# A GpSimd drain inside the routed loop of a long-convolution and mixture-of-experts kernel

## The chip, the core and the metric

The kernel runs on one core of a Trainium2 chip. A core has TensorE (PE in the profile; its weight loads are PEld), VectorE (DVE), ScalarE (ACT), GpSimd (POOL) and SyncE (SP), each with its own queue of instructions, and 16 DMA engines that all queues share. The metric is the time of the whole program on the device in microseconds (us), the median of several runs.

## What is computed

The input `x` holds 128 sequences of 32 heads, each 512 long. Each head is convolved with its own kernel, made from a state-space model, and masked to the length of its sequence. The 4096 rows that result go through a gated feed-forward layer with 16 experts of which each row uses 4, plus a shared expert that all rows use. The sum is added to `x`.

```python
y = irfft(rfft(u, n=2 * L) * rfft(K, n=2 * L)[None])[..., :L] + u * D[:, None]
y = y * mask                                    # rows of 512, 128 x 32 of them
scores = sigmoid(y @ gate_w.T) + bias
topk_w, topk_idx = top_k(scores, 4)             # normalised to a sum of one
out = sum over experts e of  cw[e] * (silu(y @ Wg[e].T) * (y @ Wu[e].T)) @ Wd[e].T
out = out + (silu(y @ Sg.T) * (y @ Su.T)) @ Sd.T
result = x + out
```

## The kernel before

The work has three stages. In the first, the convolution runs head by head on TensorE; its rows go to a table `y_rows` in HBM, and GpSimd copies `x` into `out` with 8 large transfers (line 865). In the second, the shared expert runs over 8 units of 512 rows; GpSimd adds the results into `out` with 32 indirect transfers (line 953), while VectorE works out which row goes to which expert.

The third stage is the routed loop, in which the change lies. The rows chosen for each expert are packed into tiles of 128. There are at least `NT_MIN` = 128 tiles and at most `NT` = 143; the number depends on the data, and steps from 130 on stand inside nested branches (`rest`) that are left when no tile is left. With the data of these runs, 134 tiles are computed. `turn_of(step)` writes the order of one step by hand:

- GpSimd issues the gather of the rows of tile `step + 4` from `y_rows` into one of 6 buffers `yg` (`gather`, line 894).
- TensorE transposes the rows of tile `step` (`tokens`, line 1022); ScalarE copies them out of PSUM into `yt`.
- SyncE reads whether tile `step - 2` is the first of an expert. If it is, SyncE waits until all adds issued so far have landed (line 1107), because two experts can add to the same row; then it sets a mark (`order`, line 1110).
- TensorE multiplies tile `step - 1` with the expert's gate and up weights (`inner`, line 1054) and tile `step - 2` with its down weights (`outer`, line 1080); ScalarE and VectorE do the gate in between.
- VectorE copies the result into one of 5 buffers `ob` (line 1089), and GpSimd issues an indirect transfer that adds its rows into `out` (line 1090), once the mark of the tile is set.
- SyncE issues a conditional load of an expert's weights into a ring of 8 places (line 880), for a tile six steps on.

So GpSimd's queue in this loop is an add, a gather, an add, a gather, and so on, in the order written, with nothing else between. All of its transfers are described by software on GpSimd; each one has a semaphore that tells of its landing, and the instructions that read or overwrite the data wait for that semaphore. The build closes every program with drains on all engines and a barrier between them (line 1212 in the profile), and opens it in the same way (line 1201).

The order around the change is this:

```python
turn_of(0)
unit_step(NU)
for step in range(1, NT_MIN + 2):
    turn_of(step)
```

Of the kernel before, what the change touches and what calls it, by code (L numbers as in the profile page):

```python
# [55 lines left out]
AHEAD = 4  # L56
NT = (B * H * TOPK - E) // P + E
NT_MIN = B * H * TOPK // P
QC = P // KT
WSZ = 2 * KT * I + IT * L  # L60

# [14 lines left out]
def ssm_moe_kernel(  # L76
# [15 lines left out]
    nc = tc.nc  # L92
# [39 lines left out]

    gw = const.tile([P, KT, QC], F32, tag="gw", name="gw")
    nc.gpsimd.memset(gw, 0.0)
# [24 lines left out]
    gather_q = const.tile([P, E], F32, tag="gather_q", name="gather_q")  # L159
    nc.gpsimd.tensor_add(gather_q, ident[:, :E], ident[:, QC : QC + E])  # L160
    for kt in range(2, KT):
        nc.gpsimd.tensor_add(gather_q, gather_q, ident[:, kt * QC : kt * QC + E])

# [378 lines left out]
    def gates(tb):  # L542
# [7 lines left out]
        for kt in range(KT):  # L550
            mm = nc.tensor.matmul(
                parts[kt * QC : (kt + 1) * QC],
                lhsT=gw[:, kt, :],
# [287 lines left out]
    def dep(of, on, why):  # L841
        tc.add_manual_dep(of.ins, on.ins.name, SYNC, reason=why)
# [36 lines left out]
    def load_expert(e, dst, cond=None):  # L879
        return nc.sync.dma_start(  # L880
            out=dst, in_=w_all[bass.ds(e, 1)].rearrange("o p w -> p (o w)"), cond=cond
        )
# [10 lines left out]
    def gather(t):  # L893
        nc.gpsimd.indirect_dma_start(  # L894
            out=at(yg, t),
            out_offset=None,
            in_=y_rows[:, :],
            in_offset=bass.IndirectOffsetOnAxis(ap=made["get"][:, t : t + 1], axis=0),
        )
# [71 lines left out]
    def unit_step(u):  # L971


        nonlocal gathered
        if u < NU:
            k_us[u] = nc.tensor.value_load(k_u[0:1, u : u + 1], min_val=1, max_val=KT)
            for it in range(IT):
                up(u, it, p_g, 0)
                if u == 0 and it == 0:
                    sums(NB - 1)  # L980
                    route(NB // RB - 1)
                nc.scalar.activation(sgu[it], p_g[it], AF.Silu)
                up(u, it, p_u, I)
                nc.vector.tensor_mul(at(zu, u)[:, it, :], sgu[it], p_u[it])
                if u > 0 or it > 0:
                    next(making, None)
        if u == 0:
            weights_out(NB // RB - 1)
        for q in range(TU // P):
            if u > 0:  # L990
                down(u - 1, q)
                if q % 2 == 1:
                    next(making, None)
        while "get" in made and gathered < AHEAD:
            gather(gathered)
            gathered += 1
        while "lexp0" in made and len(loads) < R - 1 and free_after(len(loads)) <= u:
            j = len(loads)
            e = nc.sync.value_load(made["lexp0"][0:1, j : j + 1], min_val=0, max_val=E - 1)
            loads.append(load_expert(e, ring_flat[:, j * WSZ : (j + 1) * WSZ]))  # L1000
# [15 lines left out]
    def tokens(t):  # L1016

        pt = at(p_t, t)

        def transposes(n):  # L1020
            for q in range(KT - n, KT):
                nc.tensor.transpose(pt[:, q, :], at(yg, t)[:, q * P : (q + 1) * P], ident)  # L1022

        if t < len(p_t):
            transposes(KT)
        else:
            by_tiles(k_ts[t], transposes)
        nc.scalar.copy(at(yt, t), pt)  # L1028
        nc.vector.scalar_tensor_tensor(  # L1029
            at(junks, t),  # L1030
            epos,
            made["texp"][:, t : t + 1],
            at(yg, t)[:, L:],
            ALU.is_equal,
            ALU.mult,
            accum_out=at(wts, t),
        )
# [6 lines left out]
    def registers(t):  # L1044
        w0s[t] = nc.tensor.value_load(
            made["woff"][0:1, t : t + 1], min_val=0, max_val=(R - 1) * WSZ
        )
        k_ts[t] = nc.tensor.value_load(made["ntk"][0:1, t : t + 1], min_val=1, max_val=KT)

    def inner(t):  # L1050
        pgu = at(p_gu, t)
        def products(n):
            for q in range(KT - n, KT):
                mm = nc.tensor.matmul(  # L1054
                    pgu,
                    lhsT=at(yt, t)[:, q, :],
                    rhs=ring_flat[:, bass.ds(w0s[t] + q * 2 * I, 2 * I)],
                    start=(q == KT - n),
                    stop=(q == KT - 1),
                )  # L1060
                in_ring(t, mm)

        by_tiles(k_ts[t], products)
        sg = at(sgs, t)
        nc.scalar.activation(sg, pgu[:, :I], AF.Silu)  # L1065
        nc.vector.scalar_tensor_tensor(  # L1066
            at(zs, t), pgu[:, I:], at(wts, t), sg, ALU.mult, ALU.mult
        )

    def turn(t):  # L1070
        for it in range(IT):
            nc.tensor.transpose(  # L1072
                at(p_z, t)[:, it, :], at(zs, t)[:, it * P : (it + 1) * P], ident
            )
        nc.vector.tensor_copy(at(zts, t), at(p_z, t))  # L1075

    def outer(t):
        po = at(p_o, t)
        for it in range(IT):
            mm = nc.tensor.matmul(  # L1080
                po,
                lhsT=at(zts, t)[:, it, :],
                rhs=ring_flat[:, bass.ds(w0s[t] + WD + it * L, L)],
                start=(it == 0),
                stop=(it == IT - 1),
            )
            in_ring(t, mm)
        ob = at(obs, t)
        nc.vector.tensor_copy(ob, po)  # L1089
        add = nc.gpsimd.indirect_dma_start(  # L1090
            out=out,
            out_offset=bass.IndirectOffsetOnAxis(ap=made["put"][:, t : t + 1], axis=0),
            in_=ob,
            in_offset=None,
            compute_op=ALU.add,
        )
        dep(add, marks[t], "the rows it adds to")
        for other in adds:
            tc.declare_no_dep(add.ins, other.ins, reason="other rows, or behind the mark")
        adds.append(add)  # L1100

    def order(t):


        new = nc.sync.value_load(made["fresh"][0:1, t : t + 1], min_val=0, max_val=1)  # L1105
        with tc.If(new > 0):
            wait = nc.sync.nop()
            for other in adds:
                dep(wait, other, "the rows they add to")
        marks[t] = nc.sync.nop()  # L1110

    with tc.manual_schedule(engines=None):

        dep(nc.tensor.nop(), parts_last[0], "in TensorE's order")
        for u in range(NU):
            unit_step(u)
        for _ in making:
            pass
        registers(0)

        def turn_of(step):
            if step + AHEAD < NT:
                gather(step + AHEAD)
            else:
                nc.gpsimd.nop()
            if step < NT:
                tokens(step)
            if step >= 2:
                order(step - 2)
                turn(step - 2)  # L1130
            if 1 <= step <= NT:
                inner(step - 1)
            if step >= 2:
                outer(step - 2)
            if step + 1 < NT:
                registers(step + 1)
            if 1 <= step < NT:

                t = step - 1
                e = nc.sync.value_load(made["lexp"][0:1, t : t + 1], min_val=0, max_val=E - 1)  # L1140
                to = nc.sync.value_load(made["loff"][0:1, t : t + 1], min_val=0, max_val=(R - 1) * WSZ)  # L1141
                go = nc.sync.value_load(made["load"][0:1, t : t + 1], min_val=0, max_val=1)  # L1142
                ld = load_expert(e, ring_flat[:, bass.ds(to, WSZ)], go)
                for other in loads:
                    tc.declare_no_dep(ld.ins, other.ins, reason="another place of the ring")
                loads.append(ld)

        turn_of(0)
        unit_step(NU)
        for step in range(1, NT_MIN + 2):  # L1150
            turn_of(step)

        def rest(step):

            if step == NT + 2:
                return
            _, (some,) = nc.values_load_multi_w_load_instructions(  # L1157
                made["full"][0:1, step - 2 : step - 1], min_val=0, max_val=1
            )
            with tc.If(some > 0):  # L1160
                turn_of(step)
                rest(step + 1)

        rest(NT_MIN + 2)

# [50 lines left out]
```

## Time and profile before

| What | Value |
|---|---|
| median of 3 runs | 943.94 us (941.65, 943.94, 944.29) |
| the profiled execution | 942.44 us |
| its span, first to last instruction | 940.7 us |
| TensorE busy | 883.1 us, 94% |
| VectorE busy | 409.3 us, 44% |
| GpSimd busy | 422.7 us, 45% |
| mean granted clock of TensorE | 0.994 |
| indirect adds in the routed loop, line 1090 | 134, 1577 ns each to issue |
| indirect gathers, line 894 | 140, 987 ns each to issue |
| transfers issued on GpSimd's queue | 314 |

An entry of the profile such as `L1090 POOL DMA_INDIRECT out<-ob,put x134 | 211.3, 1577 | 242.6 <-DVE junk L1029 214.4` reads: line 1090 of the kernel, on GpSimd, an indirect DMA that writes `out` from `ob` by the row numbers `put`, 134 times; 211.3 us busy in all, 1577 ns each; the engine was idle for 242.6 us just before these, and most of that ended when VectorE's work of line 1029 was done. An engine's name with a q (POOLq, SPq) is its sequencer: drains, waits and branches stand there and do not count as busy. A time in a row of the timeline is counted from the start of the span.

### The profile page before, as it was taken

To read this page: it belongs to the slowest core of one execution; us is meant where nothing else is said; L and a number is where in the kernel's file an instruction comes from. 1 tells how busy PE (TensorE), PEld (TensorE's weight loads), DVE (VectorE), ACT (ScalarE), POOL (GpSimd) and SP (SyncE) were. 2 spreads that over 40 slices of the span, in tenths; PEclk is the share of its full clock that TensorE was granted. 3 is DMA by queue.
4 is the path that set the end of the run, shared out by engine and by line. 5 is a ranking of instruction groups with operands and counts; after the bars stand their busy time and mean duration, and the time that the engine had idled before them with its cause. 6 is when DMAs were issued, how large, how long until landed. Compare 5 with 4: busy or idle time off the path is not lost.

```text
span 940.7 us, 14509 instructions
## 1 busy us (share of the span) xinstructions
PE 883.1 (94%) x2960; PEld 442.0 (47%) x2960; DVE 409.3 (44%) x1406; ACT 190.0 (20%) x375; POOL 422.7 (45%) x376
## 2 busy tenths in 40 slices
PE   0799997999999999999999999999999999999993
PEld 0455553444544444454444444444444444444441
DVE  7954555486950233433343334333433233344331
ACT  0122221111222122211222122212211111222220
POOL 4210000222456455655565456645655545566553
PEclk9999999999999999999999999999999999999997
DMA  4378873276769756776577567756766556667664
GB/s 163 108 253 290 293 275 137 30 249 132 184 96 233 198 111 115 138 170 116 110 135 181 114 115 126 130 101 110 134 113 114 100 106 109 109 130 138 118 114 83
DMA packets 54673, 135.95 MB, mean 145 GB/s; under 512 B 12400, under 2 KB 12560, under 8 KB 50960
## 3 DMA queue, kind: packets, MB, share of 16 engines
q0 software_dynamic: 36256, 89.77, 50.6%
q1 hardware_dynamic: 14064, 36.15, 11.3%
q10 hardware_dynamic: 4224, 8.39, 2.3%
q8 instruction: 71, 1.16, 0.5%
q14 instruction: 58, 0.48, 0.1%
HBM read 288.08 MB, written 60.64 MB: 371 GB/s over the span
## 4 chain that ended last, share of the span: by engine, by line
PE 66%; issue 1%; SPq 0%; POOL 0%; DVE 0%; ACT 0%; POOLq 0%
PE g L1054 34%; PE o L1080 24%; PE m L1022 4%; PE u L1072 3%; PE o L944 1%; POOL out L1090 0%; SPq L1157 0%; POOL yg L894 0%; SPq L1105 0%; SPq L1140 0%; SPq L1141 0%; DVE zt L1066 0%; SPq L1142 0%; ACT sgt L1065 0%; SPq L880 0%
## 5 line engine op out<-in xcount | busy, mean ns | idle before, releaser
L1054 PE MATMUL g<-store,yt 128*128 x742 | 343.0, 596 | 1.8 <-issue 1.5
L1090 POOL DMA_INDIRECT out<-ob,put x134 | 211.3, 1577 | 242.6 <-DVE junk L1029 214.4
L1080 PE MATMUL o<-store,zT 128*128 x536 | 252.2, 593 | 0.1
L1066 DVE SCALAR_TENSOR_TENSOR zt<-g,wt,sgt 128x256 f32<-128x256 f32 x135 | 65.3, 484 | 306.7 <-ACT sgt L1065 306.7
L1054 PEld LDWEIGHTS g<-store,yt 128*128 128x128 f32 x742 | 130.3, 190 | 118.7 <-issue 117.4
L1080 PEld LDWEIGHTS o<-store,zT 128*128 128x128 f32 x536 | 101.4, 190 | 129.3 <-issue 124.6
L894 POOL DMA_INDIRECT yg<-y_rows,get x140 | 138.1, 987 | 42.7 <-issue 31.7
L1089 DVE COPY ob<-o 128x512 f32<-128x512 f32 x134 | 92.7, 692 | 109.7 <-PE o L1080 101.6
L1028 ACT COPY yt<-m 128x512 f32<-128x512 f32 x136 | 79.7, 586 | 227.7 <-PE m L1022 219.3
L1065 ACT ACTIVATE sgt<-g 128x256 f32<-128x256 f32 x135 | 51.9, 384 | 268.2 <-PE g L1054 267.4
L953 POOL DMA_INDIRECT out<-ob,unit_rows x32 | 50.2, 1568 | 98.8 <-ACT ob L951 93.1
L520 PE MATMUL py<-strip,xt 128*128 128x512 f32 (+3 forms) x256 | 79.0, 447 | 7.9 <-DMA strip<-kd 7.9
L1022 PEld LDWEIGHTS m<-ident,yg 128*128 128x128 f32 x373 | 48.6, 141 | 73.1 <-issue 73.0
L1022 PE MATMUL m<-ident,yg 128*128 128x128 f32 x373 | 63.1, 273 | 1.3 <-issue 1.0
L944 PE MATMUL o<-store,z 128*128 128x512 f32 x128 | 57.7, 597 | 1.2 <-ACT yt L1028 1.2
L1075 DVE COPY zT<-u 128x256 f32<-128x256 f32 x134 | 56.3, 420 | 0.7 <-PE u L1072 0.7
L520 PEld LDWEIGHTS py<-strip,xt 128*128 128x128 f32 x256 | 42.5, 195 | 25.3 <-issue 12.3
L1072 PE MATMUL u<-ident,zt 128*128 128x128 f32 x268 | 51.2, 273 | 0.6 <-DVE zt L1066 0.6
L929 PE MATMUL g<-store 128*128 128x512 f32 x92 | 43.0, 602 | 3.1 <-issue 2.5
L865 POOL DMA_DIRECT2D out<-in_x x8 | 4.4, 558 | 88.3 <-ACT store L531 88.3
L929 PE MATMUL u<-store 128*128 128x512 f32 x92 | 42.2, 593 | 0.0
L809 DVE TENSOR_SCALAR cols<-tpos_h,stl,tok 128x143 f16<-128x143 f16 x128 | 41.8, 331 | 0.0
(272 smaller groups left out, 499.0 us busy)
## 6 DMA issues: line engine op xcount, KB each, us to landing
store<-in_w_all SPq DMA_DIRECT2D x143, 1536.0 KB
xt<-in_x_t SPq DMA_DIRECT2D x8, 1024.0 KB
y_rows<-yb ACTq DMA_DIRECT2D x8, 1024.0 KB
out<-in_x POOLq DMA_DIRECT2D x8, 1024.0 KB, 9.0
strip<-kd SPq DMA_DIRECT2D x7, 1024.0 KB
yg<-y_rows,get POOLq DMA_INDIRECT x140, 4.3
out<-ob,put POOLq DMA_INDIRECT x134, 4.8
strip<-kd SPq DMA_DIRECT2D x4, 256.0 KB
```

The source lines that it names most:

```text
L520: nc.tensor.matmul(py[:, : L - jt * P], lhsT=xt[:, jt, q, :], rhs=strip[tb][:, q, jt * P :], start=(jt == 0), stop=(jt == KT - 1),)
L894: nc.gpsimd.indirect_dma_start(out=at(yg, t), out_offset=None, in_=y_rows[:, :], in_offset=bass.IndirectOffsetOnAxis(ap=made["get"][:, t : ...
L929: nc.tensor.matmul(ps[it], lhsT=w_sh[:, c0 : c0 + P], rhs=yT[:, u, kt, :, :].rearrange("p h b -> p (h b)"), start=(kt == KT - n), stop=(kt ...
L944: nc.tensor.matmul(po, lhsT=at(zu, u)[:, it, q * P : (q + 1) * P], rhs=w_sh[:, c0 : c0 + L], start=(it == 0), stop=(it == IT - 1),)
L1022: nc.tensor.transpose(pt[:, q, :], at(yg, t)[:, q * P : (q + 1) * P], ident)
L1028: nc.scalar.copy(at(yt, t), pt)
L1054: mm = nc.tensor.matmul(pgu, lhsT=at(yt, t)[:, q, :], rhs=ring_flat[:, bass.ds(w0s[t] + q * 2 * I, 2 * I)], start=(q == KT - n), stop=(q = ...
L1066: nc.vector.scalar_tensor_tensor(at(zs, t), pgu[:, I:], at(wts, t), sg, ALU.mult, ALU.mult)
L1072: nc.tensor.transpose(at(p_z, t)[:, it, :], at(zs, t)[:, it * P : (it + 1) * P], ident)
L1080: mm = nc.tensor.matmul(po, lhsT=at(zts, t)[:, it, :], rhs=ring_flat[:, bass.ds(w0s[t] + WD + it * L, L)], start=(it == 0), stop=(it == IT ...
L1089: nc.vector.tensor_copy(ob, po)
L1090: add = nc.gpsimd.indirect_dma_start(out=out, out_offset=bass.IndirectOffsetOnAxis(ap=made["put"][:, t : t + 1], axis=0), in_=ob, in_offse ...
```

## The change

A constant is added, and ahead of step 124 (128 - 4) GpSimd gets a drain. Step 124 is six steps ahead of step 130, the first of those that may be left out. In GpSimd's queue the drain stands between the add of tile 121, the last transfer of step 123, and the gather of tile 128, the first of step 124. The other engines have the same instructions with the same waits; one or two of their unconditional branches at that step stand a few places earlier or later. Line numbers behind the change are 1 and then 3 higher.

```diff
 NT = (B * H * TOPK - E) // P + E
 NT_MIN = B * H * TOPK // P
+LAST_DRAIN = NT_MIN - 4
 QC = P // KT
...
         for step in range(1, NT_MIN + 2):
+            if step == LAST_DRAIN:
+                nc.gpsimd.drain(fusable=False)
             turn_of(step)
```

## The prediction

> **What bounds the kernel now.** I read the page first, for the balance of the engines. Its groups say what fills the routed loop, and its share row says that TensorE leads and GpSimd does not.
>
> ```profile
> PE 883.1 (94%) x2960; PEld 442.0 (47%) x2960; DVE 409.3 (44%) x1406; ACT 190.0 (20%) x375; POOL 422.7 (45%) x376
> ...
> L1054 PE MATMUL g<-store,yt 128*128 x742 | 343.0, 596 | 1.8 <-issue 1.5
> L1090 POOL DMA_INDIRECT out<-ob,put x134 | 211.3, 1577 | 242.6 <-DVE junk L1029 214.4
> ...
> L894 POOL DMA_INDIRECT yg<-y_rows,get x140 | 138.1, 987 | 42.7 <-issue 31.7
> ```
>
> TensorE is busy 94% and idles 1.8 us in all before its largest group. GpSimd issues two indirect transfers per routed tile: an add of rows into `out` (1577 ns) and a gather of rows four tiles ahead (987 ns); it idles 242.6 us before the adds. So in the loop a stall of GpSimd costs nothing until it has eaten that idle time or the lead of the gathers.
>
> Second, busy time by stretches, around the place of the change and to the end of the span (columns: length, then PE, PEld, DVE, ACT and POOL busy with counts, clock, DMA share, GB/s).
>
> ```profile
> 871.00:900.00 29.00, 28.63 (x93) 14.24 (x92) 10.47 (x31) 5.94 (x13) 15.41 (x13) 1.00 0.65 120
> 900.00:926.40 26.40, 24.32 (x66) 10.17 (x64) 9.95 (x31) 5.71 (x12) 15.40 (x12) 1.00 0.64 120
> 926.40:932.20 5.80, 0.00 (x0) 0.00 (x0) 0.66 (x1) 0.00 (x0) 1.58 (x1) 0.77 0.61 110
> 932.20:940.70 8.50, 0.00 (x0) 0.00 (x0) 0.00 (x0) 0.00 (x0) 0.00 (x0) 0.50 0.01 2
> ```
>
> TensorE is full until about 926. The last 8.5 us have no engine busy and practically no DMA (share 0.01): that stretch is not bounded by any arithmetic or transfer. What fills it stands in the instructions of the program's end (line 1212), with those of its start (line 1201) to compare, and of the exit of the last branch (line 1160). Columns: count, min/median/max in ns, first and last start in us.
>
> ```profile
> L1212 POOLq DRAIN  x3: 46/109/5623, 934.2 to 940.4; - x3
> L1212 SPq DRAIN  x3: 7/7/13, 934.4 to 940.1; - x3
> ```
>
> ```profile
> L1201 POOLq DRAIN  x1: 183/183/183, 0.4 to 0.4; - x1
> ```
>
> ```profile
> L1160 POOLq INC_SWDGE_SEM  x1: 1528/1528/1528, 932.2 to 932.2; - x1
> ```
>
> GpSimd's drain at 934.2 takes 5623 ns, the next two 109 and 46 ns, and the one at the start, before any transfer, 183 ns. The last add is issued at 927.33 and has landed by 932.2 (it takes 4.8 us), so at 934.2 there is nothing left to wait for: the 5.6 us are GpSimd's own work over something that had piled up. 314 transfers had been issued on its queue by then (8 + 32 + 134 + 140). The long drain holds the closing barrier: SyncE's drains there take 7 to 13 ns, and its last one ahead of the barrier is done by 934.52, while the barrier opens after 939.8.
>
> **The change, part by part.** Added: one drain on GpSimd's queue, ahead of step 124. Nothing is removed or re-addressed, and SyncE's queue is as it was. One or two unconditional branches of TensorE, ScalarE and VectorE at that step stand up to five instructions earlier or later, in the same number; a branch of TensorE takes 73 ns in the rows of line 1160, and I cost the move at nothing. In GpSimd's queue the drain falls between the add of tile 121 (issued at the end of step 123) and the gather for tile 128 (the start of step 124). These are the rows around it in the timeline:
>
> ```profile
> 872.38 1.58 POOL L1090 DMA_INDIRECT out<-ob,put  x1 [1.35 <-DVE junk L1029]
> 874.27 0.99 POOL L894 DMA_INDIRECT yg<-y_rows,get  x1 [0.30 <-issue]
> 875.56 1.58 POOL L1090 DMA_INDIRECT out<-ob,put  x1 [0.31 <-DVE junk L1029]
> 877.44 0.99 POOL L894 DMA_INDIRECT yg<-y_rows,get  x1 [0.30 <-issue]
> ```
>
> *The last drain.* Take its price as proportional to the transfers issued since the drain before: (5623 - 109) / 314 = 17.6 ns each. After step 124 starts, 12 adds (tiles 122 to 133) and 12 gathers (128 to 139) remain, so the last drain would cost 109 + 24 x 17.6 = 0.53 us: 5.09 us less. All of it lies on the path of the end; the ceiling is SyncE, at the barrier by 934.52, which would allow 5.3. Bounds: 0, if the price is one for any number of transfers, and 6.6, if the 1528 ns that precede it (the same instruction took 31 ns at the program's start) shrink too. I take 5.09: the drains with nothing behind them are cheap, so the price goes with what is outstanding.
>
> [...]
>
> *The added drain.* No row shows a drain between transfers in flight. At 873.95 the add of tile 121 has just been issued; it lands at 877.24 (4.86 us after its start), so a drain that waits for transfers lasts at least 3.3 us. The pass over the 290 earlier ones takes 290 x 17.6 = 5.1 us. Together: 5.2 us if the pass starts at once and the landing falls inside it, 8.5 if the pass begins only after the landing, and 0.1 if it does nothing. I take 5.2. [...]
>
> *Who waits behind it.* The gather of tile 128 starts at 879.5 instead of 874.3 and lands 4.8 later, at 884.2. TensorE reads it in step 128:
>
> ```profile
> 889.62 0.49 PE L1022 MATMUL m<-ident,yg 128*128 128x128 f32 x3
> ```
>
> So 5.4 us of cover remain, and 2.1 if the drain takes 8.5; the drain would have to last 10.6 us to hold TensorE up, and past that each us costs one. The next gather (tile 129) is needed at 894.46 and starts 3.2 us after that of 128: more cover. The adds slip too. GpSimd's shortest turn is 1.58 + 0.30 + 0.99 + 0.31 = 3.2 us, so the adds of tiles 122, 123 and 124 start at 880.8, 883.9 and 887.1 (before: 875.56, 879.28, 885.09). Tile 125 opens an expert: SyncE lets its add go only when all earlier adds have landed (889.9 before, 891.9 now), so the add of 125 goes from 891.0 to 893.0. SyncE is then 2.0 us late with its conditional weight load at 892.6, which serves a tile six steps on, some 25 us away, and it runs a step in 3.4 us where TensorE takes 4.8. The add of 126 comes at 896.2 (0.6 late), that of 127 at 900.47 as before. VectorE fills a result buffer again five tiles later, after 19 us or more: covered. The last add, at 927.33, is not moved. With an 8.5 us drain the lateness ends at tile 129, still 16 us ahead of the last add. Cost: 0.
>
> *The sum.* Against the profiled execution: 942.44 (span 940.7 and 1.74 around it) - 5.09 + 0 = 937.35. That execution lies 1.5 below the median of the runs shown; the edit is a fixed amount, so the median goes from 943.94 to 938.85, and I say 938.8, 0.54% faster. A difference over 0.3% (2.8 us) is about what a measurement of this kernel can tell from none.
>
> **The rivals.**
>
> *A fixed price.* The long drain is paid once the queue has been used at all, whatever the number, or the added one settles nothing because it meets transfers in flight. Then the end stays 5.6 us and the added drain is covered in either case: 943.9. For it: only one drain with transfers behind it is in the trace. Against it: a fixed price would need a reason to be 5.6 us with the queue empty for 2 us.
>
> *Only the newest count.* If GpSimd takes old transfers off its books while it goes on issuing, the last drain passes over fewer than 314. With 64 (a number I choose for illustration) one costs 86 ns, 24 of them 2.1 us, and the gain is 3.4: 940.5. Against it: an add takes 1577 ns from the first to the last, so nothing shows such work in the issue.
>
> *A slow pass in mid-loop (slower).* The final pass ran over idle DMA engines (share 0.01); at step 124 their share is 0.65. Were the pass slowed by that, it is exposed from 10.6 us on and eats the whole gain at 10.6 + 5.1 = 15.7 us, which is 54 ns per transfer, three times the price at the end. At 70 ns the drain takes 20.3 us, the gather of tile 128 lands 9.7 us late, and the time is 943.94 + 9.7 - 5.1 = 948.5. For it: nothing measured under load. Against it: issuing an add takes the same 1577 ns under this load throughout.
>
> **How the numbers follow.** The proportional price has a chance of 0.70, the newest-only 0.09, the fixed price 0.14, the slow pass 0.07. The first alone would lie between 936.6 and 940.4 (a gain up to 6.6, and the spread of the runs before, 941.65 to 944.29). The range of 8 in 10 is 936.6 to 943.6: nearly all of the first (0.66), the newest-only (0.09) and a part of the fixed one (0.05). Faster by over 0.3% (under 941.1): 0.69 of the first and 0.06 of the second, 0.75. Slower: the slow pass, 0.07. The rest, 0.18, is within 0.3%.
>
> **What would show it.** Right: a drain on GpSimd at about 874 of 5 to 9 us, then a last drain of about 0.5 us; the same stretch of TensorE from 871 to 926; the gather of tile 128 landed before TensorE's transposes of step 128; the adds back in their places by tile 127 or 129; the stretch after the last landing 3.4 us long instead of 8.5. Wrong: a last drain still near 5.6 us (fixed price), one of 1 to 4 us (newest only), or idle time of TensorE before line 1023 at step 128 (slow pass). A last drain that is short with an unchanged end would mean that another engine's arrival at the barrier, not GpSimd's, sets the end.

## The result, and the profile after

| | before | after |
|---|---|---|
| median | 943.33 us (940.97 to 944.29, 7 runs) | 939.95 us (938.97 to 940.43, 7 runs) |
| profiled execution: span | 940.7 us | 938.2 us |
| last landing of an add, to the end of the span | 932.12 to 940.66: 8.54 us | 933.88 to 938.24: 4.36 us |

The ratio is 0.9965, with a 95% interval of 0.9952 to 0.9977: 0.35% faster, where 0.54% was forecast.

First the instructions of the end, of the added drain (line 1153) and of the exit of the last branch in the changed kernel (count, min/median/max in ns, first and last start in us):

```profile
L1215 POOLq DRAIN  x3: 52/109/2102, 935.1 to 938.0; - x3
L1215 SPq DRAIN  x3: 7/7/13, 937.3 to 937.6; - x3
```

```profile
L1153 POOLq DRAIN  x1: 8282/8282/8282, 873.8 to 873.8; - x1
```

```profile
L1163 POOLq INC_SWDGE_SEM  x1: 660/660/660, 934.0 to 934.0; - x1
```

The last drain fell from 5623 to 2102 ns, not to 530. The instruction ahead of it, which I had left at 1528 ns, fell to 660. The added drain is entered at 873.8 while the add before it is still being issued (until 875.60), and ends at 882.08.

Next, GpSimd's timeline around the added drain, and TensorE's transposes of step 128:

```profile
874.02 1.58 POOL L1091 DMA_INDIRECT out<-ob,put  x1 [1.36 <-DVE junk L1030]
882.86 0.99 POOL L895 DMA_INDIRECT yg<-y_rows,get  x1 [7.25 <-SPq L1143]
884.15 1.58 POOL L1091 DMA_INDIRECT out<-ob,put  x1 [0.30 <-issue]
```

```profile
891.25 0.49 PE L1023 MATMUL m<-ident,yg 128*128 128x128 f32 x3
```

The queue stood still for 7.25 us. The gather behind it (tile 128) landed at 886.32 and was read at 891.25. All times of this execution were already 1.64 us later than in the execution before when the drain was reached: the add of tile 10, about 510 us earlier, is late by 1.61, and the add of tile 121 by 1.64. The routed loop runs that much earlier or later from execution to execution (in the other profiles the add of tile 5, ahead of any added drain, lies between 0.25 us early and 2.15 late). That is why the two spans differ by 2.4 us and the stretches at the end by 4.2. The add of tile 122 is late by 8.58, that of tile 129 by 1.61, and the last one by 1.63: the loop gave nothing away.

The end of the changed kernel by stretches:

```profile
926.40:933.90 7.50, 1.52 (x4) 0.38 (x2) 1.18 (x2) 0.27 (x1) 2.56 (x2) 0.83 0.74 122
933.90:938.20 4.30, 0.00 (x0) 0.00 (x0) 0.00 (x0) 0.00 (x0) 0.00 (x0) 0.50 0.01 6
```

The empty stretch is 4.3 us long where it was 8.5. What shortened it is the end, as forecast; what was mis-sized is how much of the last drain would stay (2102 ns, not 530). The experiments asked what the length of that drain goes with, and when the added one costs nothing.

### The profile page after: what moved, and what is told of

Its sections match the earlier page's. It is cut to its first block, busy times and chain, and to the rows that moved or that the text cites. A ratio compares the mean times of both kernels' runs of the same rounds, so it can differ in the third digit from the quotient of the medians.

```text
span 938.2 us, 14510 instructions
## 1 busy us (share of the span) xinstructions
PE 885.6 (94%) x2960; PEld 443.3 (47%) x2960; DVE 409.0 (44%) x1406; ACT 189.7 (20%) x375; POOL 422.6 (45%) x376
## 4 chain that ended last, share of the span: by engine, by line
PE 65%; SPq 2%; issue 1%; POOL 0%; DVE 0%; ACT 0%; POOLq 0%
PE g L1055 33%; PE o L1081 23%; PE m L1023 4%; PE u L1073 3%; PE o L945 1%; SPq L1106 1%; SPq L1141 0%; SPq L1160 0%; SPq L1142 0%; SPq L1143 0%; SPq L881 0%; POOL out L1091 0%; DVE zt L1067 0%; ACT sgt L1066 0%; POOLq L1160 0%
```

## The experiments

Three theories fitted the two drains of the result (5623 ns with 314 transfers since the drain before, 2102 with 24): a fixed part plus 12 ns each (affine), 83 ns each for only the newest (newest-only), or 17.6 ns each with a floor of 3.3 us after the last landing (floor). Moving the one drain to another step changes the number behind it, which is 272 less twice the step.

**The drain at steps 16, 64, 100 and 129.** Each is one edit, shown for step 16:

```diff
-LAST_DRAIN = NT_MIN - 4
+LAST_DRAIN = 16
```

> The one added drain stands ahead of step 16 instead of 124: 74 transfers ahead of it, 240 behind. Affine theory (1.8 us plus 12.1 ns for each transfer since the drain before, from 5623 ns for 314 and 2102 ns for 24): last drain 4.7 us; the added one about 1 us beyond the landing of the add before it, some 6 us in all. Newest-only theory (83 ns each for the newest 66): last drain 5.6 us. Floor theory (17.6 ns each, but never done before 3.3 us after the last landing): last drain 4.3 us, the added one 3.3 us beyond the landing, about 8.3 us.

> The added drain ahead of step 64: 170 transfers ahead of it, 144 behind. Affine: last drain 3.6 us, the added one about 2 us beyond the landing. Newest-only: last drain 5.6 us. Floor: last drain 2.7 us, the added one 3.3 us beyond the landing.

> The added drain ahead of step 100: 242 transfers ahead of it, 72 behind. Affine: last drain 2.7 us. Newest-only: 5.6 us, so a time near the kernel before. Floor: 2.1 us, as with step 124, and 3.3 us beyond the landing for the added one.

> The added drain ahead of step 129, the last place outside the branches: 300 transfers ahead of it, 14 behind. Affine: last drain 2.0 us. Newest-only: 1.3 us. Floor: 2.1 us. The adds have some 20 us less to catch up in than with step 124: if they do not, the last add is late and the gain shrinks from 3.4 us; if they do, the time is that of step 124 within 0.5 us (about 939.5 against 943).

Here are the last drain and the instruction ahead of it, for steps 16, 64, 100 and 129 in this order, one fence for each kernel:

```profile
L1215 POOLq DRAIN  x3: 52/109/2266, 936.6 to 939.4; - x3
...
L1163 POOLq INC_SWDGE_SEM  x1: 700/700/700, 935.4 to 935.4; - x1
```

```profile
L1215 POOLq DRAIN  x3: 52/109/4628, 933.8 to 939.0; - x3
...
L1163 POOLq INC_SWDGE_SEM  x1: 1278/1278/1278, 932.0 to 932.0; - x1
```

```profile
L1215 POOLq DRAIN  x3: 52/109/6017, 935.4 to 942.0; - x3
...
L1163 POOLq INC_SWDGE_SEM  x1: 1627/1627/1627, 933.3 to 933.3; - x1
```

```profile
L1215 POOLq DRAIN  x3: 52/109/1281, 934.8 to 936.7; - x3
...
L1163 POOLq INC_SWDGE_SEM  x1: 460/460/460, 933.9 to 933.9; - x1
```

No theory that lets the price rise with the number behind the drain all the way holds: 72 transfers cost more than 144, and 240 hardly more than 24. That fells affine and floor. Among the small numbers the price is a straight line: 14, 24 and 72 transfers take 1281, 2102 and 6017 ns, which is 82 ns each above 0.13 us. Newest-only had the slope right (1.3 us with 14), but its constant count of 66 fails for 72, 144 and 240. The instruction ahead of the drain follows a line as well: 460, 660 and 1627 ns are 20 ns each above 0.18 us.

Read backwards, each of the two lines turns a duration into a number of transfers, an estimate for every end. The lines are drawn through the rows of 14 and 24, so the other four rows are the test, and in each the two instructions agree:

| step of the drain | transfers behind it | by the drain, 82.1 ns each | by the instruction ahead, 20 ns each |
|---|---|---|---|
| 129 | 14 | 14 | 14 |
| 124 | 24 | 24 | 24 |
| 100 | 72 | 72 | 72 |
| 64 | 144 | 55 | 55 |
| 16 | 240 | 26 | 26 |
| none | 314 | 67 | 67 |

The reading that I take from these rows is that GpSimd keeps finished transfers on its books and takes some off as it goes. It is an estimate: no view of the traces shows such a count, and "on the books" below means the number that a line gives. By it the end takes about 0.10 us (82 and 20 ns) for each one left, and the kernel before had 67 of 314 left. Step 100 has 72, more than no drain at all (6017 ns against 5623), and its empty end is longer (9.07 us) than before (8.54); its single time was 944.04. Steps 16 and 64 were also timed once each, at 941.46 and 941.01, beside a kernel before that spread from 941.91 to 944.84. Single times say little there, and the argument rests on the ends. Step 129 has 14 left: 937.98 us against 943.01, a ratio of 0.9939 (0.9921 to 0.9958).

The added drains are entered before the add ahead of them has landed, so the same line can't be read off their length. At step 16, 74 transfers were issued ahead of the drain, and all can still be on the books. These are the drain and the add ahead of it:

```profile
L1153 POOLq DRAIN  x1: 8075/8075/8075, 376.0 to 376.0; - x1
```

```profile
376.19 1.60 POOL L1091 DMA_INDIRECT out<-ob,put  x1 [1.19 <-DVE junk L1030]
```

The drain ended 6.25 us after the add was issued. A pass of 74 x 82 + 130 ns that starts at the issue gives 6.2 us, which would fit. But the drains of the later experiments that have 16, 22 or 60 transfers ahead of them, since the drain before or the start, end 0.4 to 0.9 us later than such a pass and the landing allow. What fits them, this one and those with 2 is the time from the last packet of GpSimd's DMA queue, which the trace holds, to the end of the drain. With 2, 16, 22, 60 and 74 transfers it is 0.46, 1.03, 1.31, 2.83 and 3.41 us (the first two are medians of 29 drains ahead of the steps 101 to 129 and of 15 in the kernel with one at every eighth step; 22 is the second of two, at step 129, 60 the first of every eighth, at step 9): a line of 0.38 us and 41 ns for each transfer, half the slope of the drain at the end (82 ns). So these drains ended 0.46 to 3.41 us behind the last packet, later the more transfers there were. Whether there is another half that falls into the time before the last packet, the traces do not show. At step 124 the last packet came 2.90 us after the issue and the drain ended 3.58 later: by that line, 78 transfers on the books out of 290.

**The pass by transfer or by size, and one drain at step 88.** With the drain at step 112, 12 small gathers of 16 rows each go into dead space; the step of 88 is an edit like those above.

```diff
+            if LAST_DRAIN <= step < LAST_DRAIN + 12:
+                small_gather(step)
```

> One drain ahead of step 112, with 48 routed transfers behind it, and 12 more gathers of 16 rows each, one in each of the steps 112 to 123, into dead space (their data is not used). Priced by transfer: 60 of them, a last drain of 5.0 us and 1.38 us for the instruction ahead of it. Priced by rows or bytes: 48 plus 12 eighths, 49.5, a last drain of 4.2 us and 1.17 us.

```profile
L1225 POOLq DRAIN  x3: 52/109/5037, 949.7 to 955.3; - x3
```

5037 ns, and 1380 for the instruction ahead of it. The two lines give 5.06 us and 1.38 for 60 transfers, and 4.19 and 1.17 for 49.5, so here a transfer of 16 rows counted like one of 128. (Its time of 957.36 is that of a loop with 12 more gathers in GpSimd's queue, whose turn is then 4.4 us; the add of tile 98 is on time and that of tile 121 is 15 us late.)

> One drain ahead of step 88: 96 transfers behind it. If all since the drain stay on the books: last drain 0.11 + 96 x 0.082 = 8.0 us and the instruction ahead of it 2.1 us, slower than before by 3 us. If GpSimd takes some off when the books are full, somewhere over 72: a last drain between 1.0 and 6.5 us. A price for each transfer of 17.6 ns would give 1.8 us.

```profile
L1215 POOLq DRAIN  x3: 52/109/5042, 935.6 to 941.2; - x3
```

5042 ns, and 1388 for the instruction ahead of it: by both lines 60 on the books out of the 96 issued behind the drain (its single time was 943.27). With 72 behind the drain (step 100) all of them were still on. By this estimate 36 of the 96 were off.

The added drains add to the estimate, if the line of 41 ns is read backwards for them: after 170, 218, 242, 266, 278, 290 and 300 transfers the first drain of a kernel comes out at 65, 112, 31, 55, 66, 78 and 89 on the books. (Two profiles have their first drain after 242 transfers and two after 290; the pairs give 31 and 30, 78 and 79.) From 170 to 218, and from 242 to 300, the count rises by the number issued, to within one. Read so, none came off in those stretches and many in others: about 105 by 170, as many again between 218 and 242, and some 36 between 300 and the 314 of the kernel before, whose end comes out at 67. By what rule, and whether the reading is right, no run shows: behind a drain the lines have 36 off after 96 transfers, 89 after 144 and 214 after 240, which no batch of one size gives.

**The cover taken away: a drain ahead of each of the steps 100 to 129.**

```diff
-            if step == LAST_DRAIN:
+            if 100 <= step <= 129:
```

> The cover taken away: a drain ahead of each of the steps 100 to 129. If a drain holds the queue until the add before it has landed, GpSimd's turn grows from 3.2 us to about 6.4 (add 1.6, landing 3.2 more, gather 1.0, gaps 0.6), over the 3.9 to 5.7 us of TensorE's steps, and after the lead of four gathers is used up the loop runs at GpSimd's pace: 40 to 65 us slower than before. If an added drain does not hold the queue, no change but for the short end: some 5 us faster than before.

```profile
L1153 POOLq DRAIN  x30: 5424/5722/6293, 765.6 to 965.7; - x30
```

```profile
869.10 0.99 POOL L895 DMA_INDIRECT yg<-y_rows,get  x1 [3.76 <-PE g L1055]
870.39 1.58 POOL L1091 DMA_INDIRECT out<-ob,put  x1 [0.30 <-issue]
876.28 0.99 POOL L895 DMA_INDIRECT yg<-y_rows,get  x1 [4.31 <-PE g L1055]
```

1003.82 us, 60 slower. GpSimd's turn is 6.6 to 7.2 us (from gather to gather), and the loop runs at that pace; TensorE is busy for 159 of the 206 us from 765 to 971. With two transfers since the drain before, only 0.46 us of these 5.7 us lie behind the last packet, and nearly all the rest is the end of the add's issue and the time to its last packet: the drains end 3.0 to 3.6 us after the add is issued (the first of them 4.5). So a drain holds the queue, and these thirty cost 60 us without cover; the single one at step 124 had cover: the adds were 1.64 us late ahead of it, and the last one 1.63.

**A drain ahead of every eighth step.**

```diff
-            if step == LAST_DRAIN:
+            if step % 8 == 1 and step > 1:
```

> A drain ahead of every eighth step (9, 17, ... 129), sixteen instead of one; 14 transfers behind the last, as with step 129. Theory on the books (the pass costs 82 ns in the drain and 20 ns in the instruction ahead of it for each transfer still on GpSimd's books): each drain in the loop passes over 16 transfers (1.3 us) while it waits 3.2 us for the last landing, so it holds the queue some 3.3 us beyond the issue of the add instead of 6.5, and is covered even where steps are short; the stretch after the last landing is 3.2 us as with step 129, and the last add is not late: the time of step 129 or 0.7 us below it, about 5.5 us under the kernel before. Rival (each drain costs the loop something whatever it covers, as the one at step 16 cost 1.2 us): 15 more drains of 0.5 to 1.2 us each, 3 to 14 us slower than step 129.

939.63 us against 943.81, ratio 0.9957 (0.9944 to 0.9971). The last drain took 1275 ns, as with step 129, but against the execution before the adds fell behind by 1.7 us over the loop (2.15 us late at tile 0, 3.87 at the last). Most drains held the queue 3.6 to 3.9 us beyond the issue and not 3.3: the last packet came after 2.6 to 2.8, and the drain ended 1.03 later. (The third held it for 6.4, since its last packet came after 5.4.) The time lies between the two forecasts: the drains get shorter, and sixteen of them still cost 1.7 us, about 0.1 each. With the single drain at step 16 the adds had gone from 1.70 late (tile 10) to 2.92 (tile 40), 1.2 us in one place. TensorE's steps are near 3.9 us long there, and about 4.8 at step 128. That the shorter steps are why is argued, not shown.

**Two drains, ahead of steps 118 and 129, beside the changed kernel.** From step 129 alone the last add had come 0.7 us later than the loop ahead of the drain.

```diff
-            if step == LAST_DRAIN:
+            if step in (118, 129):
```

> Two drains, ahead of steps 118 and 129: 22 transfers between them, 14 behind the second. Theory on the books: the first may pass over up to some 80 transfers (6.7 us beyond the issue of the add, as at step 124) and is covered; the second passes over 22 (1.9 us, inside the wait for the landing) and holds the queue 3.3 to 3.7 us beyond the issue instead of the 6.7 of the single drain at step 129, so the last add is not late (that one lost 0.7 us): stretch after the last landing 3.2 us, 5.4 us under the kernel before, about 938. Rival (lateness of two drains adds up at the end of the loop): last add 0.7 us late or more, no better than the single drain at step 129.

> The changed kernel itself, beside the other on the same chip: stretch after the last landing 4.4 us, as before; some 3.5 to 4.2 us under the kernel before. With 10 more transfers behind its drain, 1.0 us for the pass and the instruction ahead of it, it should be about 1.2 us above the kernel with the two drains.

937.74 us against 943.41 before, ratio 0.9942 (0.9930 to 0.9955); the changed kernel on the same chip 939.50, ratio 0.9960 (0.9948 to 0.9972). Here are the two drains, and the add ahead of the second:

```profile
L1153 POOLq DRAIN  x2: 5818/6627/7436, 849.5 to 896.8; - x2
```

```profile
896.99 1.58 POOL L1091 DMA_INDIRECT out<-ob,put  x1 [1.75 <-DVE junk L1030]
```

The second drain ended 4.0 us after the issue of that add (2.7 to the last packet and 1.3 behind it), where the single one at step 129 ended 6.7 after; the lateness against the execution before is 1.17 us ahead of the two drains and 0.97 at the last add. The last drain took 1275 ns. The median with two drains is 1.8 us under that of the changed kernel (937.11 to 939.32 against 938.63 to 940.23, six runs each); against the single drain at step 129 (937.98, on another chip) the medians cannot tell.

The second profile of the changed kernel shows one thing that the first did not. These are SyncE's marks, the last of which lets the last add go, in the kernel before, in this second profile, and with two drains:

```profile
L1110 SPq EVENT_SEMAPHORE  x134: 17/17/17, 305.2 to 923.6; - x134
```

```profile
L1111 SPq EVENT_SEMAPHORE  x134: 3/17/184, 305.5 to 926.8; - x134
```

```profile
L1111 SPq EVENT_SEMAPHORE  x134: 3/17/229, 310.9 to 925.0; - x134
```

Before, the last mark was set at 923.6 and the last add went at 927.33, so the mark was 3.7 us early. In the second profile it came at 926.8, after the result had been copied (926.11), and the add followed at 927.58: SyncE held it. From tile 126 to the last, every add of that profile goes 0.80 us after its mark, so 0.80 is the distance of an add from a mark that came late. In the first profile the last add went 0.80 us after its mark too (928.2 and 928.96), but its result was copied only at 928.65, so nothing was lost. With two drains the mark came at 925.0, with the add at 928.30.

## Why the prediction was right, and where it was off

**The end.** Right in place: GpSimd's drain had held the barrier (it ended at 939.83, SyncE's at 934.52), and with a drain at step 124 it fell from 5623 to 2102 ns. That the 5.6 us were work on finished transfers was my inference, and still is: that drain began 2.1 us after the last landing, and its length went with the transfers behind the drain only up to 72. The term that was mis-sized is the price by transfer: 17.6 ns came from spreading 5.5 us over all 314, where the rows of 14, 24 and 72 rise by 82 ns each, which makes the 5623 ns the price of 67. So 24 cost 2.10 us and not 0.53: a gain of 3.52 where I had 5.09. By the signs that I had set, a last drain of 1 to 4 us speaks for the newest only, to which I gave 0.09: it assumed 64 at 86 ns and gave 2.1 us and 940.5, nearer to the truth than the form to which I gave 0.70. That its 64 lies so near the 67 is luck, since I chose it for illustration. The other two rivals are out: the price is not fixed (14 to 72 transfers cost 1.3 to 6.0 us), and the drain under load was not slow enough to show, for it ended 6.5 us after the issue, over 4 us before it would have held TensorE up.

**The instruction ahead of the drain.** I had left its 1528 ns at nothing and kept them as an outer bound. It rose with the same numbers, by 20 ns each over 14, 24 and 72 transfers, and gave 0.87 us. So part of what the drain fell short by came back here, which I had not counted on: that the total lay as near to the forecast as it did owes something to luck.

**The ceiling by SyncE.** I had it at the barrier by 934.52, with 0.2 us to spare. In the profile after, its last drain ahead of the barrier starts at 937.40, after GpSimd's ended at 937.20. SyncE comes last there and takes back 0.2. (In the second profile its drain is done 0.8 us before GpSimd's, and it takes back nothing.) The sum for the end is 3.52 + 0.87 - 0.2 = 4.2 us, which is what the two stretches differ by (8.54 - 4.36). The medians differ by 3.4. The starts of the loop that vary between executions, and SyncE's late mark (0.8 us in the second profile), can make up the rest; how much is due to each is not shown.

**The added drain.** I took 5.2 us from 873.95 with the landing inside the pass; it lasted until 6.5 us after the issue. The form was wrong: the last packet came 2.9 us after the issue, and the drain ended 3.6 us behind it. That is the form for which I had 8.5, by my estimate with 78 transfers at 41 ns in place of 290 at 17.6; so 5.2 was near by chance. The cover was right: the limit was 10.6 us, and the gather had landed 4.9 us ahead of the transposes.

**What waits behind it.** The adds were back in place by tile 129, the later of the two that I had given. The step that failed is SyncE's catching up. I had it 2.0 us late at tile 125 and soon on time; its mark for that tile came 3.7 us later than the loop, and the last one still 2.9 (4.1 and 3.6 in the second profile). In the branches its turn took some 4.2 us, no shorter than many of TensorE's steps. The expert that opens at tile 125 makes it wait for adds that the drain has made late, and in one of two profiles its mark then held the last add. With drains at steps 118 and 129 the last mark stood 3.3 us ahead of its add (925.0 and 928.30), where it had stood 3.7 before.

**The two engines' drains.** GpSimd's first drain at the end took 1275 to 6017 ns over these kernels. SyncE's drains there took 7 to 13 ns in the kernels before and after, and the same with the drain at step 16, 64, 88, 100 or 129.

## What to carry to other kernels

If GpSimd has issued many transfers, look at its drain at the program's end: here it took 5.6 us with 314 behind it, and an added drain took it to 2.1 us (step 124) or 1.3 (step 129). Count as the hold of the added one the time to the last packet and some more behind it: 2.9 and 3.6 us at step 124. Ask how late the cover allows it, and put it behind, not ahead of, a point where another queue waits for GpSimd's transfers: step 129 gave a ratio of 0.9939 to the kernel before, and step 124, ahead of such a point, 0.9965. Do not work out a price for each of a number of things from one total: here even two drains with different counts left three theories open, and it took four more to show that the price does not rise all the way to 314.

## What was not expected

- The end's cost does not rise with the number of transfers: 72 since the last drain cost 6.0 us, 240 cost 2.3, and 314 cost 5.6. With a drain in the wrong place (step 100) the end took longer than with none: 9.07 us against 8.54.
- An added drain ended 0.46 us behind the last packet with 2 transfers and 3.41 with 74, a rise of 41 ns for each, half that of the drain at the end (82 ns).
- A transfer of 16 rows cost the last drain as much as one of 128: 60 of both kinds took 5.04 us, and the line of 82 ns gives 5.06 for 60.
- The routed loop runs up to 2.4 us earlier or later between profiled executions of kernels that are the same up to there (the add of tile 5 in all twelve), most of the spread of the runs of one kernel (940.97 to 944.29); the stretch after the last landing is the better measure of such a change.
